# Attention probabilities turned by VectorE blocks and a trip through DRAM instead of by TensorE

## The chip, the cores and the metric

The kernel runs on one core of one Trainium2 chip. The metric is the device time of one execution in microseconds (us); a lower figure is better. TensorE is PE in the profile, VectorE is DVE, ScalarE is ACT, GpSimd is POOL and SyncE is SP. SyncE issues nearly all the DMAs of this kernel.

## What is computed

The input is 8 images of 192 channels and 64 x 64 pixels, float32 throughout. Two layers follow each other for every image.

Layer 0 is window attention and an MLP. The 64 x 64 pixels are cut into windows of 8 x 8, so that a window has 64 tokens, and there are 6 heads of 32 channels.

```
shortcut = layer_norm(x)
q, k, v  = shortcut @ qkv_w.T + qkv_b          # per window and head
attn     = l2norm(q) @ l2norm(k).T * temperature
kth      = 16th largest of each row of attn
attn     = softmax(where(attn >= kth, attn, -100) + rpb)
x2       = shortcut + (attn @ v) @ proj_w.T + proj_b
x2       = x2 + gelu(layer_norm(x2) @ fc1_w.T + fc1_b) @ fc2_w.T + fc2_b
```

Layer 1 is a Fourier layer and an MLP: a layer norm, a 2-D FFT of every channel, a small pointwise MLP (2 to 16 to 2, with a gelu) on every frequency, the inverse FFT, an addition, and then a layer norm and an MLP of 768 hidden units as in layer 0.

The product `attn @ v` sums over the keys. The probabilities are made with the queries on the 128 partitions and the keys along the free axis, and the product needs the keys on the partitions. So each block of probabilities must be turned, and how this is done is the subject of the change.

## The kernel before

**Tiling.** An image is worked on in 8 bands `i` of 512 pixels (8 rows, 8 windows). Attention runs on a half band `hb` at a time: 4 windows, 6 heads, 64 x 64 scores each, held as a tile `s` of 128 partitions x 768 elements. There are 8 x 8 x 2 = 128 such attention steps, 16 for each image.

**Tasks.** Every piece of work is a Python generator that yields steps with `op(engine, weight, ...)` and then records the instructions of the step. `front` (L648) loads and normalizes a band and makes q, k and v; `attention` (L823) does one half band; `back` (L946) does the projection and the first MLP; `forward`, `pointwise` and `inverse` (L1013 to L1180) do the Fourier layer by groups of 16 channels; `leave` (L1195) does the last MLP and writes the output. The Fourier layer of an image and its last MLP run beside the attention of the next image: the list `streams` (L1241) gives each kind of task a place in time and a width, and three attention steps can be under way at once.

**The planner.** `issue` (L33) decides the order. It keeps a model of each engine's clock, takes the step whose engine can begin first, adds the weight of the step and a delay when the source of a dependency is another engine (30 units from PE, 15 from the others), and counts buffers in `units`. What it decides is fixed when the program is built: on the chip each engine runs its own instructions in that order, and waits at each for what it needs. A step of 384 units, the 24 recorded matmuls of L635, takes 4.06 us in the profile, so a unit stands for about 10.6 ns.

**An attention step.** POOL or DVE scales q and k; DVE transposes them by 32 x 32 blocks (L836, tile `qkt`); PE makes the scores (L846); ACT or DVE copies them into `s`; DVE finds the 16th largest of every row and masks the rest (L874 to L883); POOL subtracts the maximum and adds the bias (L886, L888); ACT takes the exponential (L890); DVE sums (L893); POOL divides (L896). Then come the lines that the change is about: six PE transposes of 128 x 128 (L903) into a PSUM tile, one copy by ACT or DVE into the SBUF tile `at` (L910), and the product with v (L928, tile `po`), in which `at` is the moving operand.

**Buffers.** `s` and `at` share the tag `att` with 5 buffers. `ps` is PSUM, 4 buffers of two banks, used by every matmul. `ot` (1 buffer) collects the attention output of a band until `back` projects it at L956.

**SyncE's queue.** SP issues its DMAs in order. Before the change it holds the loads of the bands (`xin`, L192 and L195, three DMAs for each band) and the writes of the output (`out`, L1226 and L1228, three DMAs for each band); each waits at its place in the queue until its buffer is free or its data is there.

Of the kernel before, what the change touches and what calls it, by code (L numbers as in the profile page):

```python
# [8 lines left out]
FP = mybir.dt.float32  # L9
# [12 lines left out]
ROW = 768  # L22
# [6 lines left out]
def op(engine, weight, mode=None, get="", put="", after=None, done=None, put_too=""):  # L29
    return engine, weight, mode, get.split(), (put + " " + put_too).split(), after, done  # L30


def issue(streams, units):  # L33

    change = {"pe": 20, "act": 130, "dve": 0, "pool": 0}
    clock = {e: 0 for e in change}
    mode = {e: None for e in change}  # L40
    units = {name: [0] * n for name, n in units.items()}
    events = {}
    live = []

    def advance(task, value):
        try:
            found = task["gen"].send(value)
            while not isinstance(found, tuple):

                new = dict(task, gen=found, queue=None)  # L50
                live.append(new)
                advance(new, None)
                found = task["gen"].send(None)
            task["op"] = found
        except StopIteration:
            live.remove(task)
            if task["queue"] is not None:
                start(task["queue"])

    def start(queue):  # L60
        if queue[0]:
            gen, place = queue[0].pop(0)
            task = {"gen": gen, "queue": queue, "urgency": 360 * place, "last": (None, 0)}
            queue[1] += 1
            task["order"] = (queue[1], len(live), place)
            live.append(task)
            advance(task, None)

    for tasks, width in streams:
        queue = [list(tasks), 0]  # L70
        for _ in range(width):
            start(queue)
    while live:
        best, ready = {}, {}
        for task in live:
            engines, weights, kind, get, put, after, done = task["op"]
            if isinstance(engines, str):
                engines, weights = (engines,), (weights,)
            free = 0
            deps = [task["last"]] if after is None else after  # L80
            deps = [d if d[0] is None or d[0] in change else events.get(d) for d in deps]
            if any(d is None for d in deps):
                continue
            short = False
            for name in set(get):
                n = get.count(name)
                if len(units[name]) < n:
                    short = True
                    break
                free = max(free, sorted(units[name])[n - 1])  # L90
            if short:
                continue
            found = []
            for engine, weight in zip(engines, weights):
                begin = max(clock[engine], free)
                for source, end in deps:
                    if source is not None and source != engine:
                        end += 30 if source == "pe" else 15
                    begin = max(begin, end)
                new = kind and mode[engine] and kind != mode[engine]  # L100
                cost = change[engine] if new else 0
                found.append((begin + cost + weight, engine, begin, cost, task, weight))

            _, engine, *rest = min(found, key=lambda f: f[0] + 40 * (f[1] == "dve"))
            ready.setdefault(engine, []).append((engine, *rest))
        for engine, found in ready.items():
            first = min(begin + cost for _, begin, cost, *_ in found) + 15
            best[engine] = min(
                [
                    (  # L110
                        begin + cost + task["urgency"] - 100 * ("ps" in task["op"][4]),
                        task["order"],
                        f,
                    )
                    for f in found
                    for _, begin, cost, task, _ in [f]
                    if begin <= first
                ],
                key=lambda v: v[:2],
            )  # L120
        choice = min(best.values(), key=lambda v: (v[2][1], v[:2]))[2]
        engine, begin, change_cost, task, weight = choice
        _, _, kind, get, put, after, done = task["op"]
        for name in get:
            units[name].remove(min(units[name]))
        end = begin + change_cost + weight
        clock[engine] = end
        if kind:
            mode[engine] = kind
        for name in put:  # L130
            units[name].append(end + 15)
        task["last"] = (engine, end)
        if done:
            events[done] = (engine, end)
        advance(task, (engine, end))
# [3 lines left out]
def kernel(  # L139
# [18 lines left out]
    nc = tc.nc  # L158
# [4 lines left out]
    sb = ctx.enter_context(tc.tile_pool(name="sb", bufs=1))  # L163
# [4 lines left out]
    def psum(name):  # L168
        return psp.tile([128, 2, 512], FP, tag="ps", name=name)


    ATT_BUFS, H_BUFS, XT_BUFS = 5, 7, 4
    units = dict(
        ps=4, xt=XT_BUFS, xn=1, qk=1, vv=2, att=ATT_BUFS, qkt=1, sm=2, ot=1, hn=2, xa=2,
        h=H_BUFS, xf=1, fa=1, fz=2, fo=1, xy=2,
    )

    xins = {}
# [1 line left out]
    def strip(tag, bufs, name):  # L180
        return sb.tile([128, ROW], FP, tag=tag, name=name, bufs=bufs)
# [37 lines left out]
    ident = ctile("ident", [128, 128])  # L219
# [193 lines left out]
    fo = ctile("fo", [128, 16 * U])  # L413
# [136 lines left out]
    def flat(name):  # L550
        return psum(name).rearrange("p k n -> p (k n)")
# [94 lines left out]
    xts, qks, vvs, nrms, ots, held = {}, {}, {}, {}, {}, {}  # L646
# [170 lines left out]
    def copy(done, to, of):  # L817

        (nc.scalar.copy if done[0] == "act" else nc.vector.tensor_copy)(to, of)  # L819

    EITHER = ("act", "dve")

    def attention(b, i, hb):  # L823

        nm = f"{b}_{i}_{hb}"
        scaled = yield op(("pool", "dve"), (195, 140), after=[("front", b, i, hb), "rpb"])
        qk, vv, nrm = qks[b, i][:, hb], vvs[b, i][:, hb], nrms[b, i][:, hb]
# [7 lines left out]
        qkt = sb.tile([128, 12, 64], FP, tag="qkt", name=f"qkt_{nm}", bufs=1)  # L835
# [6 lines left out]
        for h3 in range(3):  # L842
            for c in range(2):
                for wi in range(4):
                    rows = slice(32 * wi, 32 * wi + 32)
# [7 lines left out]
        s = sb.tile([128, 3, 4, 64], FP, tag="att", name=f"s_{nm}", bufs=ATT_BUFS)  # L853
        for k in range(2):
            done = yield op(EITHER, (49, 56), put="ps")
# [39 lines left out]
        yield op("pool", 150, put="sm")  # L895
        nc.gpsimd.tensor_tensor(s, s, row(rsum), ALU.mult)  # L896

        yield op("pe", 65, "full", get="ps att", put="att")
        pt = flat(f"at_{nm}")
        for h3 in range(3):  # L900
            for p in range(2):
                k = 2 * h3 + p
                nc.tensor.transpose(  # L903
                    pt[:, k * 128 : (k + 1) * 128],
                    s[:, h3, 2 * p : 2 * p + 2, :].rearrange("p w k -> p (w k)"),
                    ident,
                )
        moved = yield op(EITHER, (80, 96), put="ps")
        at = sb.tile([128, 3, 2, 128], FP, tag="att", name=f"at_{nm}", bufs=ATT_BUFS)
        copy(moved, at.rearrange("p h a t -> p (h a t)"), pt[:, :ROW])  # L910

        if hb == 0:
            yield op("pe", 53, "v", get="ps ot", put="att", after=[moved, ("vv", b, i)], done=("ot", b, i))
            ots[b, i] = strip("ot", 1, f"ot_{nm}")
        else:
            yield op("pe", 53, "v", get="ps", put="att " + held[b, i][1], after=[moved, ("ot", b, i)])
        po = psum(f"po_{nm}")
        for p in range(2):
            for h in range(6):
                c, h3 = h // 3, h % 3  # L920

                places = [(32 * h, p * 64, 0, 64)] if h < 4 else [
                    (64 * r + 32 * (h - 4), 128 + p * 32, 32 * r, 32) for r in range(2)
                ]
                for to, col, q0, n in places:
                    for w2 in range(2):
                        rows = slice(64 * w2, 64 * w2 + 64)
                        nc.tensor.matmul(  # L928
                            po[to : to + 32, w2, col : col + n],
                            vv[rows, p, h * 32 : h * 32 + 32],  # L930
                            at[rows, h3, p, c * 64 + q0 : c * 64 + q0 + n],
                            start=True,
                            stop=True,
                        )
# [11 lines left out]
    def back(b, i):  # L946

        nm = f"{b}_{i}"
# [36 lines left out]
        pair = lambda t, j: xt[:, j, t * C : (t + 1) * C]  # L985
        acc, last = yield from mlp(pair, f"b{nm}", wfc1, fcb[:, 0, :], wfc2, biased)
        ready = [last, ("biased", b, i)]
        yield op("dve", 98, put="ps xt", get="xy" if i == 0 else "", after=ready)
        if i == 0:
            xys[b] = (  # L990
                sb.tile([128, 2, 2, 8, C], FP, tag="xy", name=f"xy_{b}", bufs=2),
# [346 lines left out]
```

## Time and profile before

| | |
|---|---|
| median of 3 runs | 4787.68 us (4782.2 to 4788.69) |
| the profiled execution | 4796.72 us, its span 4794.9 us |
| mean granted TensorE clock | 0.979 |
| busy: PE / PE weight loads | 4545.6 us (95%) / 3633.2 us (76%) |
| busy: DVE / ACT / POOL | 2532.9 (53%) / 2663.2 (56%) / 2364.8 us (49%) |
| instructions | 143562 |
| DMA traffic | 63.87 MB, 13 GB/s on average |

The span runs from the first to the last instruction of one execution. A row of the profile gives source line, engine, operation, output and input tile with their shapes, and then the busy time of the group, the mean duration of one instruction in ns, and the idle time of the engine just before them with what ended it. A float32 matmul is recorded as two matmuls, a transpose as one. Matmuls overlap in the pipeline, so the duration of one is longer than the step from one to the next.

### The profile page before, as it was taken

Reading aid. Unit: us, or ns where it says so; the run is one execution under the profiler, and the core shown is the slowest. Engines: PE = TensorE matmul, PEld = TensorE weight load, DVE = VectorE, ACT = ScalarE, POOL = GpSimd, SP = SyncE. Lnnn points to the kernel's source line nnn. Section 1 sums busy time; section 2 is a strip of 40 time slices with the busy share of each in tenths; the row PEclk is TensorE's granted clock in tenths of the full one; section 3 lists DMA queues with packets and bytes.
Section 4 is the critical chain, followed back from the end, with each engine's and each line's share of the span. In section 5 each row is a group of like instructions: output and inputs, shape, how many; then the busy total and the mean of one; then the engine's idle time right before and its main releaser. Section 6 shows DMA issues by size and latency. Waiting matters only on the chain.

```text
span 4794.9 us, 143562 instructions
## 1 busy us (share of the span) xinstructions
PE 4545.6 (95%) x61898; PEld 3633.2 (76%) x61898; DVE 2532.9 (53%) x10479; ACT 2663.2 (56%) x3896; POOL 2364.8 (49%) x2189
## 2 busy tenths in 40 slices
PE   6787999999999999999999999999999999999989
PEld 4676777877778776887778876788767887778768
DVE  6776656455664567454655546645556454662111
ACT  4455666446664656555655556545566456553553
POOL 6677455445544446454555545536455455451100
PEclk8888999999999999999999999999999999999999
DMA  2000000000000000000000000000000000000000
GB/s 57 11 8 12 6 9 9 21 18 6 12 9 18 18 9 9 11 21 15 6 9 17 18 12 9 9 18 15 12 9 9 24 12 9 6 5 17 9 5 24
DMA packets 54100, 63.87 MB, mean 13 GB/s; under 512 B 17583, under 2 KB 36218, under 8 KB 53466
## 3 DMA queue, kind: packets, MB, share of 16 engines
q1 hardware_dynamic: 53454, 54.68, 3.8%
q8 instruction: 487, 7.98, 0.7%
q14 instruction: 147, 1.20, 0.1%
q10 hardware_dynamic: 12, 0.00, 0.0%
HBM read 29.29 MB, written 25.17 MB: 11 GB/s over the span
## 4 chain that ended last, share of the span: by engine, by line
PE 78%; POOL 7%; DVE 7%; ACT 5%; issue 2%; SPq 0%; DMA 0%; ACTq 0%; POOLq 0%; DVEq 0%
PE mo_d L635 10%; PE mo_b L635 10%; PE mh_d L589 7%; PE fh L1099 7%; PE fo L1126 6%; PE mh_b L589 6%; PE mh_d L602 4%; PE mh_b L602 3%; POOL nrm L738 3%; PE pq L754 3%; ACT fh L1082 3%; PE pp L956 2%; PE fy L1174 2%; PE po L928 2%; PE fb L1147 2%
## 5 line engine op out<-in xcount | busy, mean ns | idle before, releaser
L1082 ACT ACTIVATE fh<-fh,ab 128x1024 f32<-128x1024 f32 x768 | 813.1, 1111 | 395.1 <-PE fh L1099 392.5
L738 POOL TENSOR_TENSOR nrm<-nrm,mhalf 128x24 f32<-128x24 f32 x128 | 558.3, 4362 | 10.7
L886 POOL TENSOR_TENSOR s<-s,top 128x768 f32<-128x768 f32 x128 | 191.6, 1496 | 724.1 <-DVE s L883 445.0
L635 PE MATMUL mo_b<-wfc,h_b 128*128 128x192 f32 x3072 | 522.4, 328 | 0.3 <-ACT fh L1082 0.2
L635 PE MATMUL mo_d<-wmlp,h_d 128*128 128x192 f32 x3072 | 516.0, 327 | 1.3 <-ACT fh L1082 1.3
L635 PEld LDWEIGHTS mo_b<-wfc,h_b 128*128 128x128 f32 x3072 | 500.4, 191 | 10.0 <-issue 3.7
L635 PEld LDWEIGHTS mo_d<-wmlp,h_d 128*128 128x128 f32 x3072 | 498.1, 190 | 11.4 <-issue 5.8
L1099 PE MATMUL fh<-fz,w1p 32*128 32x248 f32 (+1 forms) x6144 | 461.0, 404 | 20.3 <-ACT fh L1082 14.7
L1099 PEld LDWEIGHTS fh<-fz,w1p 32*128 32x128 f32 x6144 | 291.2, 186 | 149.2 <-issue 77.6
L1126 PE MATMUL fo<-fh,w2p 128*32 128x264 f32 (+1 forms) x6144 | 380.0, 383 | 7.8 <-ACT fh L1082 5.6
L589 PE MATMUL mh_b<-hn_b,wfc_a 128*128 128x256 f32 x1536 | 376.5, 392 | 10.8 <-ACT xt L819 4.8
L589 PE MATMUL mh_d<-hn_d,wmlp_a 128*128 128x256 f32 x1536 | 366.5, 386 | 0.5 <-ACT hn_d L819 0.3
L573 ACT ACTIVATE h_d<-mh_d,fcb 128x512 f32<-128x512 f32 x384 | 241.1, 686 | 214.7 <-PE mh_d L602 179.3
L589 PEld LDWEIGHTS mh_b<-hn_b,wfc_a 128*128 128x128 f32 x1536 | 283.7, 192 | 76.9 <-issue 25.8
L589 PEld LDWEIGHTS mh_d<-hn_d,wmlp_a 128*128 128x128 f32 x1536 | 283.0, 191 | 56.2 <-issue 19.1
L896 POOL TENSOR_TENSOR s<-s,rsum 128x768 f32<-128x768 f32 x128 | 200.0, 1567 | 236.6 <-DVE rsum L894 191.1
L876 DVE MATCH_REPLACE8 s<-top,s 128x64 f32<-128x64 f32 x1536 | 309.6, 209 | 0.0
L1126 PEld LDWEIGHTS fo<-fh,w2p 128*32 128x32 f32 x6144 | 185.3, 110 | 158.8 <-issue 30.2
L874 DVE MAX8 top<-s 128x8 f32<-128x64 f32 x1536 | 256.7, 208 | 51.0 <-ACT s L819 50.6
L1212 DVE TENSOR_TENSOR zt<-mo_d,xy 128x768 f32<-128x768 f32 x64 | 61.2, 957 | 413.1 <-PE mo_d L635 306.4
L878 DVE MAX8 top<-s 128x8 f32<-128x64 f32 x1536 | 265.3, 214 | 0.0
L573 ACT ACTIVATE h_b<-mh_b,fcb 128x512 f32<-128x512 f32 x384 | 241.3, 691 | 38.5 <-PE mh_b L602 27.6
(218 smaller groups left out, 8763.7 us busy)
## 6 DMA issues: line engine op xcount, KB each, us to landing
xin<-in_x SPq DMA_DIRECT2D x64, 256.0 KB
out<-z SPq DMA_DIRECT2D x64, 256.0 KB
xin<-in_x SPq DMA_DIRECT2D x128, 64.0 KB
out<-z SPq DMA_DIRECT2D x128, 64.0 KB
wfc<-in_wfc SPq DMA_DIRECT2D x1, 576.0 KB
wmlp<-in_wmlp SPq DMA_DIRECT2D x1, 576.0 KB
wfc_a<-in_wfc SPq DMA_DIRECT2D x1, 384.0 KB
wfc_b<-in_wfc SPq DMA_DIRECT2D x2, 192.0 KB
```

The source lines that it names most:

```text
L573: nc.scalar.activation(h[:, k].rearrange("p (t n) -> p t n", t=2), ph[:, :, k * HALF : (k + 1) * HALF], AF.Gelu, bias=fc1_bias[:, 2 * fp + ...
L589: nc.tensor.matmul(ph[:, t, k * HALF : (k + 1) * HALF], w1[0][:, f], hn[:, t * HALF : (t + 1) * HALF], start=(first and k == 0), stop=not ...
L602: nc.tensor.matmul(ph[:, t, k * HALF : (k + 1) * HALF], w1[1][rows, f], hn[rows, BAND:ROW], start=(first and k == 0), stop=not first, skip ...
L635: nc.tensor.matmul(acc[:, j, t * C : (t + 1) * C], hs[f // 2][:, f % 2, q * 128 : (q + 1) * 128], w2[:, f, ORDER[t]], start=(f == 0 and t ...
L738: nc.gpsimd.tensor_tensor(nf, nf, mhalf[:, :24], ALU.pow)
L874: nc.vector.max(best[:, 0:8], of)
L876: nc.vector.match_replace(s2, best[:, 0:8], of, -3.0e38)
L878: nc.vector.max(best[:, 8:16], s2)
L896: nc.gpsimd.tensor_tensor(s, s, row(rsum), ALU.mult)
L1082: nc.scalar.activation(hs[hf, k], ph, AF.Gelu, bias=ab[:, 0:1])
L1099: nc.tensor.matmul(phs[k // 2][:, k % 2, cols], w1p[i][rows, hf].rearrange("p h v -> p (h v)"), fz[rows, :] if rhs is None else zu[rows, : ...
L1126: nc.tensor.matmul(po[rows, :] if i == 0 else pou[rows, :, 1 : U - 1], w2p[i][:, hf].rearrange("p a v -> p (a v)"), hs[hf, k // 2][:, k % ...
```

## The change

Image 0 keeps the old way (`turned_by_pe`, the old lines in a function of their own). For images 1 to 7, 112 of the 128 attention steps, `turned_by_dma` is used. VectorE transposes the 32 x 32 blocks of `s` in two instructions of 128 x 384 elements into a tile `tt`. A block then is right in itself, but lies in the wrong quarter of the partitions. SyncE writes each quarter of 32 partitions to a scratch tile `rows` in DRAM, with rows of 192 elements, in four DMAs, and reads the whole tile back with one DMA of 128 partitions x 768 elements into `at`. The product with v reads `at` through the function `keys`, in runs of 32 elements.

The planner learns of SP as an engine: the four writes count 220 units, the read 45, and what SP has issued arrives 210 units later. `tt` and `at` take `att` buffers, the DRAM scratch has 3 buffers (`turn`). `ot` gets two buffers instead of one, and a step of `back` is made to wait in the planner until the tile that it writes to (`xy`) has been made.

```diff
-    change = {"pe": 20, "act": 130, "dve": 0, "pool": 0}
+    change = {"pe": 20, "act": 130, "dve": 0, "pool": 0, "sp": 0}
+    arrives = {"pe": 30, "sp": 210}
...
-                        end += 30 if source == "pe" else 15
+                        end += arrives.get(source, 15)
...
-            units[name].append(end + 15)
+            units[name].append(end + (150 if engine == "sp" else 15))
...
-    ATT_BUFS, H_BUFS, XT_BUFS = 5, 7, 4
+    ATT_BUFS, H_BUFS, XT_BUFS, TURN_BUFS = 5, 7, 4, 3
...
-        ps=4, xt=XT_BUFS, xn=1, qk=1, vv=2, att=ATT_BUFS, qkt=1, sm=2, ot=1, hn=2, xa=2,
-        h=H_BUFS, xf=1, fa=1, fz=2, fo=1, xy=2,
+        ps=4, xt=XT_BUFS, xn=1, qk=1, vv=2, att=ATT_BUFS, qkt=1, sm=2, ot=2, hn=2, xa=2,
+        h=H_BUFS, xf=1, fa=1, fz=2, fo=1, xy=2, turn=TURN_BUFS,
...
+    def turned_by_dma(s, nm):
+        yield op("dve", 108, get="att turn", put="att")
+        tt = sb.tile([128, 4, 2, 3, 32], FP, tag="att", name=f"tt_{nm}", bufs=ATT_BUFS)
+        for p in range(2):
+            nc.vector.transpose(
+                tt[:, :, p].rearrange("q g h k -> q h g k"),
+                s[:, :, 2 * p : 2 * p + 2, :].rearrange("q h w (e k) -> q h (w e) k", k=32),
+            )
+        yield op("sp", 220, put="att")
+        rows = dram.tile([128, 4, 192], FP, tag="at", name=f"ar_{nm}", bufs=TURN_BUFS)
+        to = rows.rearrange("(g k) c n -> c k g n", k=32)
+        for c in range(4):
+            part = tt[32 * c : 32 * c + 32].rearrange("q g p h k -> q g (p h k)")
+            nc.sync.dma_start(to[c], part)
+        moved = yield op("sp", 45, get="att", put="turn")
+        at = sb.tile([128, 4, 2, 3, 32], FP, tag="att", name=f"at_{nm}", bufs=ATT_BUFS)
+        nc.sync.dma_start(
+            at.rearrange("q c p h k -> q (c p h k)"), rows.rearrange("r c n -> r (c n)")
+        )
+        def keys(rows, h3, p, q0, n):
+            return at[rows, q0 // 32 : (q0 + n) // 32, p, h3, :]
+        return moved, keys
...
+        if b == 0:
+            moved, keys = yield from turned_by_pe(s, nm)
+        else:
+            moved, keys = yield from turned_by_dma(s, nm)
...
-            ots[b, i] = strip("ot", 1, f"ot_{nm}")
+            ots[b, i] = strip("ot", 2, f"ot_{nm}")
...
-                            at[rows, h3, p, c * 64 + q0 : c * 64 + q0 + n],
+                            keys(rows, h3, p, c * 64 + q0, n),
...
+        if i > 0:
+            ready.append(("xy", b))
```

## The prediction

> **What bounds the kernel now.** I read the busy shares and the slices first, then the chain of waits, then the table by stage, and last the groups and waits of the lines that the change touches.
>
> ```profile
> PE 4545.6 (95%) x61898; PEld 3633.2 (76%) x61898; DVE 2532.9 (53%) x10479; ACT 2663.2 (56%) x3896; POOL 2364.8 (49%) x2189
> ...
> PE   6787999999999999999999999999999999999989
> ...
> PE 78%; POOL 7%; DVE 7%; ACT 5%; issue 2%; SPq 0%; DMA 0%; ACTq 0%; POOLq 0%; DVEq 0%
> ```
>
> PE is nearly always busy from the fifth slice on, and the chain that ended last runs through PE for 78% of the span. The first four slices are the start and image 0, where PE waits, and there the change leaves the turning alone. The table by stage gives the steady part (busy PE, PEld, DVE, ACT, POOL):
>
> ```profile
> 600.00:4320.00 3720.00, 3609.49 (x50355) 2889.64 (x50352) 2047.18 (x8499) 2144.39 (x3113) 1915.30 (x1766) 0.99 0.04 12
> ```
>
> From 600 to 4320 us, which holds images 1 to 7 but for their edges, PE is busy 3609.5 of 3720 us, 97%, at a granted clock of 0.99, and no other engine is over 58%. Here a microsecond taken from PE is a microsecond of the span, as long as the others keep up. The lines that go, and a stretch of the timeline that holds one of them:
>
> ```profile
> L903 PE MATMUL at<-ident,s 128*128 128x128 f32 x768 | 112.5, 287 | 61.3 <-POOL s L896 56.7 <-ACT fh L1082 2.2 <-POOL xf L1022 1.7
> L819 ACT COPY at<-at 128x768 f32<-128x768 f32 x115 | 91.0, 799 | 166.0 <-PE at L903 165.8
> ...
> 1149.31 1.99 PE L589 MATMUL mh_b<-hn_b,wfc_a 128*128 128x256 f32 x8
> 1151.14 0.82 PE L903 MATMUL at<-ident,s 128*128 128x128 f32 x6
> 1151.89 1.93 PE L1126 MATMUL fo<-fh,w2p 128*32 128x264 f32 x32
> ```
>
> The six transposes stand 0.82 us in the trace, but the next group starts 0.75 us after them. Of the 61.3 us of idle time before them most is in image 0: from 600 to 4320 us the waits of PE read
>
> ```profile
> PE at L903 <- POOL s L896: 5.2, 11, 0.6
> ...
> PE at L903 <- ACT fh L1082: 2.2, 1, 2.2
> ```
>
> **The change, part by part.** The order of the changed program has 672 PE transposes fewer (112 steps x 6) and 112 copies fewer, so it does what it says.
>
> *PE, removed.* From start to start of the next group, six transposes take 0.66 to 0.75 us where the timeline shows them (4291.57 - 4290.91 = 0.66; 1087.71 - 1087.00 = 0.71; 0.75 above). I take 0.70: 112 x 0.70 = 78.4 us. Their weight loads, 72.9 us for 624 in the steady part, give the same, 117 ns x 672 = 78.6. Low end 112 x 0.66 = 74; high end the busy time, 88.08 us for 624 there, 141 ns x 672 = 95. All of it lies on the path. PE's changes between kinds of matmul hardly move (1995 in the order before, 2022 after), so nothing is put down for them.
>
> *PE, its waits before L903.* 5.2 + 2.2 + 0.6 (POOL `rs_b`) = 8 us go with them. What is late next is `po`, see below.
>
> *ACT and DVE.* About 100 ACT copies of 799 ns and 11 DVE copies of 957 ns go. DVE gains 224 transposes of 128 x 384. The nearest row is
>
> ```profile
> L836 DVE STREAM_TRANSPOSE qkt<-qk x128: 920/979/1020, 35.5 to 4269.2; 128x768 f32<-128x768 f32 x128
> ```
>
> By size half of 979 ns, 0.49 us, so 0.98 us for each step and 110 us in all; if it were all fixed cost, 219 us. DVE goes from 55% to at most 60% of the steady part. Cost nothing, hidden behind PE; but the 0.98 us stands in the chain of one attention. The order also has 8 table loads more on ACT (193 to 201, 1283 ns each, 10 us), hidden at 58% busy.
>
> *Moving operand of `po` in runs of 32.* The row for L1054 (`fz`, 32x132 in four runs of 33) has a mean of 284 ns, that of L1029 (132 in one run) 288. No cost.
>
> *`ot` with two buffers, `xy`.* No PE wait before names either; nothing.
>
> *SP and the DMAs: the new wait.* On PE the product `po` now waits for the read-back, and everything behind it on PE waits too. No row shows this route, so I bound it from the queue's own timeline.
>
> ```profile
> 65.56 1.31 SPq L433 DMA_DIRECT2D frow<-in_fwd  x4
> 68.31 1.89 SPq L435 DMA_DIRECT2D frow<-frow  x3
> ...
> 1.18 1.21 SPq L195 DMA_DIRECT2D xin<-in_x  x2
> ...
> 3.54 1.09 PE L658 MATMUL lt<-ident,xin 128*128 128x128 f32 x4 [3.54 <-DMA xin<-in_x]
> ...
> 4791.51 1.10 SPq L1228 DMA_DIRECT2D out<-z  x2
> ```
>
> Issue: an issue takes 0.33 us (8 partitions, `frow`) to 0.6 us (`xin`, 64 partitions); four writes 1.3 to 2.4 us, I take 2.0. Landing of the writes: `frow<-frow` needs what `frow<-in_fwd` brings and starts 68.31 - 66.87 = 1.44 us after the last issue; for writes to DRAM the end of the kernel bounds it, 4794.9 - 4792.61 = 2.3 us; I take 1.9. Read-back: the first `xin` load, 256 KB, issued at 0.72 us, lets PE start at 3.54, 2.8 us with its issue; for 384 KB I take 3.0 and bounds 2.7 and 3.3. Sum 6.9 us from the end of the DVE transposes, bounds 5.4 and 8.0.
>
> Cover: the planner lets `po` start no sooner than 220 + 210 + 45 + 210 = 685 units after the transposes, 7.3 us at 10.6 ns. I counted in the order how much PE work, by the busy times of the rows, stands between the last `tt` transpose and the first `po` of each of the 112 steps: lowest 3.3 us, median 8.4, tenth from the top 13.6. Against a route of 5.4 us the shortfalls add up to 5 us, against 6.9 to 20, 8 to 58, 9 to 114, 10 to 192. The count leaves out a group that is running when it begins (up to 4.1 us), so I take half of the 20: +10 us. On SP, the route's own DMAs queue behind an `out` or `xin` in only 14 of 112 steps, 0.34 + 1.10 us each: 20 us at most if all of it were exposed; I put it inside the 10 and the bounds. The other way round, the loads and outputs now queue behind turns; each `xin` is loaded two bands ahead, so a few us hide.
>
> The Trainium skill, "VectorE: DVE Perf Modes", Rules for kernel authors, speaks against the change: it would do a 128 x 128 transpose on TensorE where a PSUM result will do, and keep VectorE for single 32 x 32 blocks. That rule is about the step alone; this trace prices that step at 0.70 us of the engine that bounds. "DMA: Bandwidth & Descriptors", Anatomy of one DMA, gives about 2 us of fixed cost for each DMA plus bytes at 436 GB/s: were the five paid one after another, an estimate from that page is 4 x 2.2 + 2.9 = 11.7 us, and the same count would give some 340 us of stalls and 5040 us in all. The four `frow` issues in 1.31 us and their common landing 1.44 us later speak for paying it twice, not five times.
>
> **Sum.** -78.4 - 8 + 10 = -76 us: the profiled 4796.7 us becomes 4720, and against the median, which lies 9 us lower, 4787.7 - 76 = 4711 us. Own range of this case: best -95 - 8 + 5 = -98, 4690; worst -74 + 37 (the count at 7.5 us) = -37, 4751.
>
> **The rivals.** (1) *The turn takes longer than its cover; slower.* Place: PE at `po`, in order, all else behind it. The gain of 86 us is used up when the shortfalls reach 86, by the count at a route of 8.5 us; at 10 us it is 4788 - 86 + 192 = 4894 us. For it: half of the read-backs stand less than 3.2 us of PE work ahead of their `po`, and writes of 768-byte rows to DRAM that are read back at once occur nowhere in the trace. Against: all rows add up to 6.9, and the planner's gap is 7.3. (2) *Part of it comes back as waits.* From 600 to 4320 us PE and its loader waited 24 times for POOL's `s`: those chains had no slack. The chain grows from about 1.9 us (transposes and copy) to 0.98 + 6.9 = 7.9, by 6.0; if the new order hides half of the 24, 12 x 6.0 = 72 us return: 4788 - 86 + 72 = 4773 us. Against: the PE work between the first and the last `po` of an image does not grow in the new order (image 4: 519 before, 508 after). (3) *No change:* another engine sets the pace and PE idles for what it saves: 4788 us. Against: none is over 60%.
>
> **Chances.** The forecast 0.64, (2) 0.17, (3) 0.04, (1) 0.15. The range takes in the forecast's own and (2): 4690 to 4778. Faster by over 0.2% (9.6 us, about what this measurement can tell): 0.64 + 0.17 = 0.81; within 0.2%: 0.04; slower: 0.15.
>
> **What would show it.** Right: L903's successor with 96 transposes and some 14 us; PE busy lower by 75 to 100 us at about 97% of the steady part; `po <- DMA at` on PE's waits at 10 to 40 us in all; 112 turns on SP with about 2 us of issue, and about 7 us from DVE's transpose to landing. Wrong: `po <- DMA at` above 86 us (rival 1), or PE idle spread over scores and `po` while DVE or ACT run late (2, 3). A median above 4751 breaks the sum, one above 4778 the prediction.

## The result and the profile after

The changed kernel takes 4870.27 us (median of 4 runs, 4863.18 to 4876.07) against 4788.18 us for the kernel before: a ratio of 1.0172 [1.0158, 1.0186], 82 us slower. The forecast was 4711, the range 4690 to 4778. The profiled execution took 4863.18 us, its span is 4861.4 us.

The busy shares, the slices and the chain of waits of the changed kernel:

```profile
PE 4516.1 (93%) x61226; PEld 3588.5 (74%) x61226; DVE 2612.9 (54%) x10688; ACT 2586.6 (53%) x3806; POOL 2364.2 (49%) x2190
...
PE   6787989999989999999999999999999999999989
...
PE 67%; DVE 9%; POOL 8%; DMA 5%; ACT 5%; issue 3%; SPq 2%; ACTq 0%; POOLq 0%; DVEq 0%
```

PE has 672 matmuls fewer, as planned, and still the span is longer. Its share of the chain falls from 78% to 67%, and DMA and SP's queue, which had none, now hold 7%. The steady part (busy PE, PEld, DVE, ACT, POOL, granted clock, DMA share, GB/s) and the waits of PE in the whole span (total, times, longest):

```profile
600.00:4320.00 3720.00, 3524.52 (x48896) 2798.69 (x48890) 2089.81 (x8515) 2041.92 (x2980) 1889.29 (x1737) 0.98 0.12 34
```

```profile
PE po L969 <- DMA at<-ar: 114.7, 64, 5.3
PE at L835 <- POOL s L946: 48.3, 8, 12.1
PE s L896 <- DVE qkt L886: 24.1, 12, 5.0
```

PE is busy for 94.7% of the stage instead of 97%, DVE rises by one point to 56%, ACT and POOL fall: the bound did not move to another engine. The first wait is new and the largest. The second is the wait before image 0's own transposes, which stays.

One turn, in the timeline of the changed kernel (start, duration, engine, line):

```profile
636.77 1.04 DVE L852 STREAM_TRANSPOSE tt<-s 128x384 f32<-128x384 f32 x2 [1.65 <-POOL s L946]
637.84 1.77 SPq L861 DMA_DIRECT2D ar<-tt  x4
...
641.27 0.34 SPq L864 DMA_DIRECT2D at<-ar  x1
...
641.77 1.16 PE L1104 MATMUL fz<-fa,frow 32*128 32x132 f32 x28
...
644.25 0.80 PE L969 MATMUL po<-at,vv 64*32 64x64 f32 x64 [1.33 <-DMA at<-ar]
```

DVE ends at 637.81; four issues take 1.77 us; the read-back is issued 1.66 us after the last of them, when the writes have landed; `po` starts 2.98 us later. That is 6.44 us from the end of the transposes, about the forecast route of 6.9. But PE had nothing left ahead of `po` at 642.92, 5.1 us after the transposes, and stood 1.33 us. The planner's order put too little work between.

Over all 112 turns, from the trace: the median from the end of DVE's transposes to PE's being ready for `po` is 7.1 us, the tenth from below 4.7, the lowest 2.2. Against a route of 6.7 us (0.03 + 1.78 of issue + 1.60 to the read-back + 3.27 to `po`, medians) 47 of the 112 are short, by 65 us together. The other 50 us or so of the waits come from turns that take longer than 6.7 us. In 35 turns the read-back is issued over 4 us after the transposes instead of 3.4: in 14 of these another turn's writes and read-back stand between on SP (with loads or outputs too in 5), in 4 loads or outputs (once with a read-back), in 17 no other DMA of SP. These 17 turns hold 33 us of PE's waits before `po`, and they have one thing in common. The profile lists a DMA queue that brings instructions, in packets of up to 16 KB (packets, MB, share of the DMA engines):

```profile
q8 instruction: 482, 7.90, 0.7%
```

In all 17 such a packet was in flight between the first write and the read-back; of the 72 other turns with nothing of SP between, 22 had one, and of the 50 turns without such a packet none was late. In 11 of the 17 the writes landed 2.8 to 3.5 us after the last issue instead of 1.6; in the other 6 they landed in time, but one issue took 1.2 to 2.2 us instead of 0.44. No experiment below changes these packets, so this is a coincidence in time that was seen and not a cause that was tested.

The waits do not end the account. The views by stretch around one wait of 2.50 us for the read-back (stretch, length, busy engines, granted clock), and the timeline there:

```profile
605.00:617.80 12.80, 7.71 (x188) 5.07 (x181) 12.70 (x60) 8.46 (x13) 8.71 (x10) 1.00 0.31 94
617.90:624.70 6.80, 6.01 (x177) 4.76 (x166) 2.44 (x3) 1.73 (x4) 3.31 (x2) 0.50 0.02 5
624.80:640.00 15.20, 15.20 (x126) 11.38 (x126) 4.92 (x16) 11.88 (x16) 3.31 (x5) 1.00 0.07 19
```

```profile
617.35 0.86 PE L969 MATMUL po<-at,vv 64*32 64x64 f32 x64 [2.50 <-DMA at<-ar]
...
621.91 2.09 PE L1149 MATMUL fh<-fz,w1p 32*128 32x264 f32 x16
...
627.49 1.15 PE L1149 MATMUL fh<-fz,w1p 32*128 32x264 f32 x16
```

The clock falls to 0.50 for 6.8 us right after the wait, and sixteen matmuls of the same kind take 2.09 us in it and 1.15 us behind it. So a wait costs more than its length. I split each span into PE's idle time, the loss by the clock (half of the half-clock time in which PE was not idle), and the rest, which is PE's work at full clock (us, profiled executions):

| kernel | span | PE idle | half-clock time (loss) | rest | of the idle: `po` for the DMA |
|---|---|---|---|---|---|
| before | 4794.9 | 241.1 | 198.3 (69.0) | 4484.8 | none |
| after | 4861.4 | 336.8 | 294.2 (110.8) | 4413.8 | 114.7 (64 times) |
| difference | +66.5 | +95.7 | (+41.8) | -71.0 | |

The loss by the clock is an estimate: it counts work at the half clock as half as fast, where the sixteen matmuls above took 1.8 times as long. By this split the saving is real, 71 us of PE's work; idle time takes back 96 us and the clock 42.

### The profile page after: what moved, and what is told of

Its sections match the earlier page's. It is cut to its first block, busy times and chain, and to the rows that moved or that the text cites. A ratio compares the mean times of both kernels' runs of the same rounds, so it can differ in the third digit from the quotient of the medians.

```text
span 4861.4 us, 143631 instructions
## 1 busy us (share of the span) xinstructions
PE 4516.1 (93%) x61226; PEld 3588.5 (74%) x61226; DVE 2612.9 (54%) x10688; ACT 2586.6 (53%) x3806; POOL 2364.2 (49%) x2190
## 4 chain that ended last, share of the span: by engine, by line
PE 67%; DVE 9%; POOL 8%; DMA 5%; ACT 5%; issue 3%; SPq 2%; ACTq 0%; POOLq 0%; DVEq 0%
PE mo_d L640 10%; PE mo_b L640 9%; PE mh_d L594 6%; PE fh L1149 6%; PE fo L1176 5%; PE mh_b L594 5%; POOL nrm L743 4%; PE mh_d L607 3%; DMA at<-ar 3%; PE pq L759 3%; PE mh_b L607 2%; DMA ar<-tt 2%; ACT fh L1132 2%; PE po L969 2%; PE fy L1224 2%
## 5 line engine op out<-in xcount | busy, mean ns | idle before, releaser
L1149 PE MATMUL fh<-fz,w1p 32*128 32x264 f32 (+1 forms) x6144 | 465.5, 407 | 8.7 <-ACT fh L1132 3.7
L578 ACT ACTIVATE h_d<-mh_d,fcb 128x512 f32<-128x512 f32 x384 | 241.1, 685 | 227.7 <-PE mh_d L607 177.6
```

Source lines behind the costliest of these rows:

```text
L578: nc.scalar.activation(h[:, k].rearrange("p (t n) -> p t n", t=2), ph[:, :, k * HALF : (k + 1) * HALF], AF.Gelu, bias=fc1_bias[:, 2 * fp + ...
L1149: nc.tensor.matmul(phs[k // 2][:, k % 2, cols], w1p[i][rows, hf].rearrange("p h v -> p (h v)"), fz[rows, :] if rhs is None else zu[rows, : ...
```

## The experiments

My theory was that the planner's numbers leave too little work between the turn and `po`. Rivals: that loads and outputs on SP's queue make the turn late; that the added DVE work and DMA traffic slow the other engines; that `ot` and `xy` changed the order for the worse. All kernels are the changed kernel but for the edit shown, and a ratio is to the kernel before, run again beside them.

**A later arrival in the planner.** What I had missed in `issue`: `arrives` is added only where `source != engine`. The read-back's source is SP itself, so the landing of the writes counts for nothing, and 210 is added once, ahead of `po`: the planner asks for 220 + 45 + 210 = 475 units, 5.0 us, not 685 (15 more between DVE and SP are left out here, as in the prediction). Two kernels raise this to 320 + 45 + 280 = 645 (6.8 us) and 320 + 45 + 480 = 845 (9.0 us).

```diff
-    arrives = {"pe": 30, "sp": 210}
+    arrives = {"pe": 30, "sp": 280}        # e1_plan; 480 in e2_margin
-        yield op("sp", 220, put="att")
+        yield op("sp", 320, put="att")
```

> Only two planner numbers change: the four writes count 320 units instead of 220, and what SP has issued arrives 280 units later instead of 210, which is what the trace of the changed kernel shows (3.4 us from the first write issue to the read-back issue, 3.3 us from there to the product). Theory A (the plan leaves 220 + 45 + 210 = 475 units, about 5 us, for a route of 6.7 us, and every stall of PE costs again through a halved clock): the waits of the product for the read-back fall from 115 us to about 40, half-clock time from 294 us to about 240, and the time to about 4770 us. Rival B (what hurts is that the writes queue behind the loads and outputs on SP and on the DMA rings): waits stay above 90 us and the time above 4840 us. Rival C (the longer chain paces the images whatever the plan says): the time stays within 10 us of 4870.

> As the run before, with the arrival at 480 units: a cover of 320 + 45 + 480 = 845 units, 9 us, 2 us more than the clear route. Theory A: waits for the read-back below 20 us, half-clock time back near 210 us, time 4715 to 4740 us, faster than the kernel before. Rival B: waits of 60 us or more remain from obstructed turns, 4800 us. Rival C: the product moved later delays back and the next image, PE idles elsewhere, 4850 us or more.

Measured: with 280, 4725.65 us, ratio 0.9863 [0.9847, 0.988]; with 480, 4737.72 us, 0.9885 [0.987, 0.9899]. Two integers turn a loss of 1.7% into a gain of 1.4%, 44 us more than theory A expected of the first. PE's waits, first with 280, then with 480:

```profile
PE po L969 <- DMA at<-ar: 43.6, 33, 3.6
PE s L896 <- DVE qkt L886: 20.1, 10, 5.0
```

```profile
PE s L896 <- DVE qkt L886: 39.7, 21, 5.0
PE po L969 <- DMA at<-ar: 17.6, 12, 3.4
```

With 280 the waits for the DMA fall from 114.7 to 43.6 us. With 480 they fall to 17.6, but the scores now wait 20 us longer for `qkt`, probably because the attention steps are held for longer and the next ones start late. The kernel with 280 beats both given ones and is the fastest of all, level with a later one at 4726.47, but for the one below that leaves the trip out.

**The other DMAs off SP's queue.** The loads of images 1 to 7 and all outputs go through ScalarE's queue.

```diff
-        nc.sync.dma_start(xa, rows[0:CA])
+        (nc.sync if b == 0 else nc.scalar).dma_start(xa, rows[0:CA])
...
-        nc.sync.dma_start(rows[0:CA], z[:, 0:BAND].rearrange("p (r s) -> p r s", s=HW))
+        nc.scalar.dma_start(rows[0:CA], z[:, 0:BAND].rearrange("p (r s) -> p r s", s=HW))
```

> The planner as in the changed kernel; the loads of images 1 to 7 and all outputs are issued by ScalarE instead of SyncE, so that nothing but turns stands in SP's queue. Theory A: only the part of the waits that obstructed turns cause can go, at most 50 of 115 us; time 4800 to 4850 us. Rival B: waits below 40 us, time 4770 us or less. Rival C: no change, 4870 us, or more since ScalarE has 0.34 to 0.6 us of issue for each DMA.

Measured: 4921.18 us, 1.027 [1.0255, 1.0285], slower still, where theory A expected 4800 to 4850.

```profile
PE po L969 <- DMA at<-ar: 123.6, 61, 6.9
```

The wait stays with SP's queue free of everything but turns, and 42 turns, not 35, have the read-back issued over 4 us after the transposes; so the place of the loads and outputs in SP's order was not what made the wait in this order. In 15 of them a DMA of another turn stands between (SP keeps its order, and a turn's writes stand behind the read-back of the turn before it, which waits for landing), in 27 none. Of these 27, 22 had an instruction packet in flight, and the other 5 the packets of a load or an output, which now come from ACT's queue but move beside the turn's own as before. ACT now spends 192 us on issuing, and PE waits 30 us instead of 22 for its `xt` and `xa`; that may be part of the extra 51 us, but was not taken apart.

**No trip.** The DMAs and SP's steps are left out and `po` reads the blocks where DVE left them, so that the output is not the one wanted and the time alone is of use.

```diff
-        yield op("dve", 108, get="att turn", put="att")
+        moved = yield op("dve", 108, get="att", put="att")
...
-        yield op("sp", 220, put="att")
...
-        moved = yield op("sp", 45, get="att", put="turn")
...
+        at = tt
```

> The trip through DRAM is left out: the product reads the VectorE blocks where they lie, so the output is not the reference's. PE work, VectorE work and copies are those of the changed kernel. Theory A and rival B: without the trip nothing is left to wait for, PE keeps its gain of 71 to 78 us, 4700 to 4720 us. Rival C: the chain through VectorE or the new order is at fault, 4760 us or more.

Measured: 4652.45 us, 0.9708 [0.9694, 0.9723]. The steady part:

```profile
600.00:4320.00 3720.00, 3653.62 (x50569) 2930.29 (x50571) 2137.34 (x8772) 2118.58 (x3081) 1933.09 (x1802) 1.00 0.04 13
```

PE is busy 98.2% of it at a clock of 1.00, with no half-clock time at all, and the rest is 4408.8 us, 76 below before. So everything that the change loses is lost through the trip, with the time and the buffer that it takes; even the idle time, 197.7 us, is less than before's 241.1, which is why the time is below the 4700 to 4720 us that were expected. Against this floor the kernel with 280 still pays 73 us (4725.65 - 4652.45), by the split 53 of idle time and 20 of clock.

**Only `ot` and `xy`.** All images are turned by PE.

```diff
-        if b == 0:
+        if b >= 0:
             moved, keys = yield from turned_by_pe(s, nm)
```

> The changed kernel with all images turned by PE: of the change only the second buffer of ot and the planner's wait on xy are left. Theory A: nothing in the trace waits for ot, so the time is that of the kernel before within 10 us, and PE idle stays near 241 us. Rival D (the new order that these two give is itself part of the loss or the gain): 20 us or more away from the kernel before, either way.

Measured: 4780.63 us, 0.9978 [0.9969, 0.9988]: 11 us faster than the kernel before, so it is not the cause of a loss. The next experiment, with one `ot` buffer again but the planner's wait on `xy` kept, gains 7 us; how the 11 divide between `ot`, `xy` and the luck of a new order is not shown.

**DVE's work and the trip beside the old way.** The kernel before, with PE's transposes kept; DVE's transposes and the five DMAs are added for images 1 to 7 in a task `beside`, with a buffer of their own, and nothing reads what they bring. The planner counts 320 units and an arrival of 280 for them, and `ot` has one buffer.

```diff
+        if b > 0:
+            yield beside(s, nm)
         moved, keys = yield from turned_by_pe(s, nm)
```

> The kernel before with the PE transposes kept and used; beside them VectorE's block transposes and the whole trip through DRAM run for images 1 to 7 into a buffer that nothing reads. It adds 224 VectorE transposes (120 us of VectorE) and 88 MB of DMA traffic, and takes nothing away. Theory A: PE waits for none of it, so 4790 to 4810 us. Rival E (traffic or VectorE's extra work slows the others): 4840 us or more, with longer mean times of the same instructions.

Measured: 4783.85 us, 0.9988 [0.9979, 0.9997].

```profile
600.00:4320.00 3720.00, 3614.80 (x50169) 2893.20 (x50169) 2131.08 (x8694) 2139.46 (x3095) 1919.55 (x1762) 0.99 0.12 34
```

The DMA share is 0.12 as in the changed kernel, and PE's busy time is that of before. Traffic of 34 GB/s and 1.04 us more of DVE for each step cost nothing that this run shows. The order is a new one here too, so some 20 us of cost could hide in it (two good orders below differ by 27), but not the 82 us: what costs is that PE must wait for them.

**The planner told of SP's other work.** The kernel with 280, where loads and outputs count as steps of 135 units on SP; and the same with an arrival of 360.

```diff
+    def loading(b, i):
+        yield op("sp", 135)
+        load_band(b, i)
...
-        yield op("act", 120, put="ps hn")
+        yield op("act", 120, put="ps")
...
+        yield op("sp", 135, put="hn")
```

> e1_plan, and the planner also knows that a band's load and an output take SyncE 135 units (1.44 us) each, so that it places them in SP's order against the turns. Theory A with a part of rival B (what is left of the waits, 44 us, is mostly turns behind loads and outputs): waits for the read-back 15 to 30 us, time 4695 to 4715 us. Rival (the rest is thin cover at places where PE has nothing else): waits stay at 40 us or above, 4720 to 4735 us.

> e7_sp with the arrival at 360 instead of 280 units, 0.85 us more cover. Theory A: waits for the read-back below 20 us, but the longer chain gives back some idle time at the scores as e2_margin did (40 us there); 4700 to 4725 us. Rival: the more cover the better, below 4690 us.

Measured: 4726.47 us, 0.987 [0.9853, 0.9886], and 4739.11 us, 0.9895 [0.988, 0.9909].

```profile
PE po L973 <- DMA at<-ar: 44.6, 29, 3.3
```

```profile
PE po L973 <- DMA at<-ar: 6.4, 7, 1.4
```

The first is the same as without it (44.6 us of waits against 43.6), not the 4695 to 4715 us expected. The trace of the kernel with 280 shows why: in its order only 2 turns have a load or an output between their DMAs on SP, and neither has a wait, so there was nothing to gain. In the second the wait is nearly gone, and yet it is slower, 14 us above what theory A of that run allowed: its idle time is 243.4 us, only 11 less than in the first, and its half-clock time rises from 185.1 to 225.6 us. The idle time moves elsewhere.

**The planner as I had read it.** The changed kernel's own numbers, with the arrival counted between SP's writes and its read-back too: 685 units.

```diff
-                    if source is not None and source != engine:
+                    if source is not None and (source != engine or engine == "sp"):
```

> The changed kernel with its own numbers, 220, 45 and 210, but the planner adds the arrival of 210 units also between SyncE's writes and SyncE's read-back, as the prediction took it to do; the changed kernel adds a delay only when the source is another engine. The cover grows from 475 to 685 units, 5.0 to 7.3 us, against a clear route of 6.7 us. Theory A: waits for the read-back fall from 115 us to 30 to 50, half-clock time from 294 to about 200 us, time 4715 to 4740 us, near the forecast. Rival F (that step of the reading was not what mattered): above 4800 us.

Measured: 4770.67 us, 0.9969 [0.9958, 0.998].

```profile
PE po L969 <- DMA at<-ar: 50.2, 30, 9.1
```

So between these two orders the missed condition is worth 100 us (4870 - 4771), with all other numbers as they were; how much of it is the cover and how much the luck of a new order this run alone can't tell. Theory A expected 4715 to 4740 us: even as I had read it the planner would have given a gain of 17 us, not 76.

**Does the time follow the planner's number?** Three more covers: 320 + 45 + 240 = 605, 220 + 45 + 140 = 405, and 320 + 45 + 320 = 685 units.

```diff
-    arrives = {"pe": 30, "sp": 210}
+    arrives = {"pe": 30, "sp": 240}        # e10_240, with writes at 320
+    arrives = {"pe": 30, "sp": 140}        # e12_thin, with writes at 220
+    arrives = {"pe": 30, "sp": 320}        # e13_320, with writes at 320
```

> e1_plan with the arrival at 240 instead of 280 units: a cover of 605 units, 6.4 us, just below the clear route. Theory A: between the changed kernel (475 units, 4870 us) and e1_plan (645 units, 4726 us), near the second: waits 50 to 70 us, 4730 to 4770 us. Rival F: no order between cover and time.

> The changed kernel with the arrival at 140 instead of 210 units: a cover of 405 units, 4.3 us, less than before. Theory A: waits for the read-back 160 to 220 us, half-clock time above 350 us, 4930 to 5000 us. Rival F: within 20 us of 4870.

> As the kernel with SP's writes at 320 and an arrival of 280, the arrival alone raised to 320: the planner asks for 320 + 45 + 320 = 685 units, about 7.3 us, after DVE's transposes. Theory A (the time follows the cover in steps that the planner's number sets smoothly): it lies between the kernels with 280 (4726 us) and 480 (4738 us), 4720 to 4740, waits of po for DMA 20 to 45 us, waits of scores for qkt 20 to 40 us. Theory B (each number gives a wholly new order, and that order's own luck is worth some tens of us, as the kernel with 240 showed): anything from 4710 to 4850; the waits for DMA together with the half-clock time still tell the time, each us of wait costing 1.3 to 1.5 us. A time under 4720 would be the fastest of the real versions.

Measured: 605 units 4846.48 us, 1.0126 [1.0111, 1.0141]; 405 units 4860.37 us, 1.0154 [1.0137, 1.0171]; 685 units 4744.04 us, 0.99 [0.9883, 0.9917]. The waits, in this order:

```profile
PE po L969 <- DMA at<-ar: 110.0, 45, 9.4
```

```profile
PE po L969 <- DMA at<-ar: 111.8, 56, 5.6
```

```profile
PE po L969 <- DMA at<-ar: 32.6, 25, 3.9
```

The first two missed: 605 units lie near the good 645, but the kernel is 121 us slower than that one and only 24 us better than 475, and 405 units are no worse than 475. Put side by side:

| planner's units | time | tt to PE ready, median | turns under 6.7 us | wait for the DMA | PE idle | clock loss |
|---|---|---|---|---|---|---|
| 405 | 4860 | 7.1 | 43 | 111.8 | 331.5 | 114.8 |
| 475 (after) | 4870 | 7.1 | 47 | 114.7 | 336.8 | 110.8 |
| 605 | 4846 | 8.8 | 40 | 110.0 | 321.0 | 99.2 |
| 645 | 4726 | 7.9 | 25 | 43.6 | 250.6 | 64.9 |
| 685 (counted between writes and read-back) | 4771 | 8.4 | 11 | 50.2 | 267.6 | 76.6 |
| 685 (320 + 45 + 320) | 4744 | 8.5 | 7 | 32.6 | 250.0 | 68.2 |
| 845 | 4738 | 10.8 | 1 | 17.6 | 247.1 | 73.8 |

All six orders that ask for 645 units or more (the two with SP's other work, of 645 and 725 units, are not in the table) lie at 4726 to 4771 us, all four that ask for 605 or fewer, the queue experiment included, at 4846 to 4921. The clear route of 6.7 us is 632 units of 10.6 ns and lies between. The time follows the idle time and the clock loss of PE, which fall by 105 us together between 605 and 645 units. Among the good orders the wait for the DMA alone doesn't rank them: 685 units (320 + 45 + 320) wait 11 us less than 645 and are 18 us slower, 4 us above what theory A of that run allowed. The planned gap sets them only roughly: each number makes a new order of the whole program, and the chip's gaps scatter around the planned one (at 605 units from -0.9 to 26.6 us). At 605 units one place of the order does much of the harm. The third turn of each of images 3 to 7 waits 9.1 to 9.4 us, 46 of the 110 us in all; one of the five (the end of DVE's transposes at 1542.44, then `po`):

```profile
1541.42 1.03 DVE L852 STREAM_TRANSPOSE tt<-s 128x384 f32<-128x384 f32 x2
...
1550.69 1.06 PE L969 MATMUL po<-at,vv 64*32 64x64 f32 x64 [9.12 <-DMA at<-ar]
```

PE had run out of other work 0.9 us before DVE was done, and three output DMAs on SP's queue put off the writes by 1.4 us. Of this order's turns 24 have loads or outputs between their DMAs on SP, with 66 of the 110 us, against 2 with none at 645 units: so what stands on SP matters in one order and not in another. Why the planner leaves PE nothing at that place stays open, as does why the two orders at 685 units differ by 27 us and why the rest, PE's work at full clock, is 20 us larger in both of them than at 645.

## Why the prediction was wrong, step by step

**PE, removed: right, a little high.** 78.4 us forecast, bounds 74 to 95; by the rest in the split 71.0 us in the changed kernel, just under the bounds, 76 without the trip, 81 at 645 units, and 61 to 81 over all orders. Image 0's 96 transposes are there with 17.6 us, not 14, and PE's matmuls are 672 fewer.

**DVE's transposes and the route: right.** 0.49 us forecast for 128 x 384, 538 ns measured as the median, and the 1.04 us stay hidden; 6.9 us forecast for the route, bounds 5.4 to 8.0, 6.7 measured.

```profile
L861 SPq DMA_DIRECT2D ar<-tt x448: 302/437/2177, 393.4 to 4368.1; - x150
L852 DVE STREAM_TRANSPOSE tt<-s x224: 523/538/580, 392.4 to 4366.2; 128x384 f32<-128x384 f32 x112
```

Writes and read-back were paid as two trips, not five: the reading of the Trainium skill, "DMA: Bandwidth & Descriptors", Anatomy of one DMA, as 11.7 us for five DMAs one after another was rightly set aside; the page gives its figure for DMAs that GpSimd issues, and SyncE issues these. SP's queue was sized right too: 14 turns have loads or outputs between their DMAs, as counted, 9 of them among the 35 late ones, and they hold 24 us of the waits against 20 at most by the prediction.

**Moving operand, ACT and DVE: right; `ot` and `xy`: at most 11 us better than nothing.** The `po` matmuls of the kernel without the trip, which read runs of 32, have a mean of 212 ns, those of before 215.

**The cover: wrong, and this is the step that failed.** The prediction said that "the planner lets `po` start no sooner than 220 + 210 + 45 + 210 = 685 units after the transposes, 7.3 us". It lets it start after 475, 5.0 us, because a delay is added only between different engines, as the section on the planner itself says. The sum did not use the 685; it took the waits from the count of PE's work in the order, and the 685 units lent that count their trust. The term of the sum that failed is "+10", the waits of `po` for the read-back: 114.7 us stand in its place. Three steps led to it.
- The count from the order gave a median of 8.4 us of PE work between `tt` and `po`, lowest 3.3; the chip shows 7.1 and 2.2. It summed busy times of rows, and matmuls overlap, which is the likely reason why it came out 1.3 us high (not tested). By the prediction's own table a cover 1.1 us shorter, which is as a route of 8 us instead of 6.9, has 58 us of shortfall instead of 20; the trace has 65.
- "so I take half of the 20: +10 us" went the wrong way: the shortfall is three times the 20, not half.
- A constant route was assumed; turns that other DMAs in SP's order, a slow issue or a late landing made longer add the other 50 us.

The forecast for the profiled execution was -76 us, measured are +66.5, a miss of 143: PE's work 7 (-71.0 for -78.4), its idle time 94 (+95.7 for -8 + 10) and the clock 42. The 8 us of waits that were to go with L903 did go: PE's idle time for all else than the read-back fell by 19 us. The worst case of the sum left these 8 us out, -74 + 37, where the best case had them; with them it is 4743 us instead of 4751.

**The clock: a term that was missing.** The 42 us of clock loss had no line in the sum, though before's clock of 0.99 in the steady part was quoted. Without it the change would have been 25 us slower in the profiled execution (-71.0 + 95.7), with it 66.5.

**The rivals.** Rival 1's sign and place were right, its mechanism half right: the waits exceeded the gain, yet at a route of 6.7 us, far below the 8.5 us from which it was to decide, since the cover was shorter (65 us), and only for the rest the turn longer (50). Its 4894 came near by another way: 115 us of waits and 42 of clock instead of 192. The sign that was named for it, `po <- DMA at` above 86 us, is what the profile shows. Rival 2 (4773) is near what the planner as I had read it gives (4771), by coincidence: there 50 of the 268 us of idle time are waits for the read-back and not for POOL's `s`. A chance of 0.15 for rival 1 leaned on "the planner's gap is 7.3", a number taken from a line that was not followed through.

**The rule against the change.** VectorE's 32 x 32 blocks with a trip through DRAM do beat TensorE's 128 x 128 transposes here, by 1.4% at 645 units: the rule of "VectorE: DVE Perf Modes", Rules for kernel authors, prices the step alone, while here PE is the bound. But of the 140 us between before and the kernel without the trip (4791.95 - 4652.45 in the same runs) the trip takes back 73 even then.

## What to carry to other kernels

Work that leaves the bounding engine is worth its time only if what it is replaced by arrives before that engine needs it: measure the gap in the order that results, turn by turn and at its low end, not its median, and read the planner's condition for every edge, also those within one engine. A wait on TensorE is to be priced with the clock behind it. Where a planner's number fixes the order, try several: here 605, 645 and 685 units gave 4846, 4726 and 4744 us, and no sum here told them apart.

## What the runs showed of the hardware

TensorE's clock halves after shorter waits than I would have looked for. In the steady part of the changed kernel there are 26 half-clock stretches of 3.4 to 10.2 us, 133 us in all, against 12 with 41 us before and none in the kernel without the trip. In all 38 PE was idle for 1.2 to 3.4 us of the 3.4 us ahead. Gaps of 0.5 to 1 us seldom bring one (2 of 47 in the changed kernel, counted when the clock falls in the gap or within 2 us behind it); of gaps of 1.5 us and more 23 of 34 do, before 8 of 15, but none of 7 in the kernel without the trip. The Trainium skill, "TensorE: Matmul & The Clock Gate", section "HAM oscillation — how this bites in real kernels", gives the rule that gaps of more than about 3.4 us are to be avoided; these runs show that 1.5 us can be enough. The stretches are whole multiples of 3.4 us, which agrees with the window of 3413 ns that the same page states in its section "What's actually happening".

The trip through DRAM meets packets that no line of the kernel issues, those that bring instructions: of the turns with nothing else of SP between, 17 of 39 with such a packet in flight were late, and none of 50 without. In the kernel with 280 it is 23 of 51 and none of 46.
